# Row sums inverted in a compact tile by way of memory, part of their addition on GpSimd; norms, first taps and q/k scaling on ScalarE

## The chip, the cores and the metric

One core of a Trainium2 chip runs the whole kernel as one program. The metric is the device time of one execution in microseconds (us), less is better. The core has five engines with an instruction stream each: TensorE (PE in the profile; PEld is its weight load), VectorE (DVE), ScalarE (ACT), GpSimd (POOL) and SyncE (SP), which here only issues DMAs, all of them in one queue, in order. The engines meet through semaphores that the framework places. SBUF holds the tiles, PSUM the results of the matmuls, DRAM the inputs, the output and a few intermediate tiles.

## The reference, cut to what matters

x is (8, 256, 32, 32) in fp32: 8 images, 256 channels, 1024 positions. Four layers, each added to its input, x = x + layer(group_norm(x)):

```python
# layer 0: attention, 8 heads of 64; q and k of unit length over the head's channels
q, k, v = split(w_qkv @ gn(x));  q = q/|q|;  k = k/|k|
o = softmax(10 * q^T k) v;  y = w_out @ o + b_out
# layers 1 and 2: 3x3 convolution, 256 -> 256 channels, padding 1
# layer 3, after a layer norm over channels; 4 branches of 64 channels:
xm = mamba(xn) + skip_scale * xn       # causal conv of 4 taps, silu, 16-state scan over 1024 steps
g  = sigmoid(qpw @ conv3(xm));  xg = g * xm
R  = rpw @ conv3(xg) + xg
xm2 = fpw @ conv3(cat(xs, R)) + xs
out = gelu(layer_norm(fc @ cat(conv3(xm2), mha(xm2))))   # mha: 8 heads of 32 channels
out = proj @ layer_norm(dwconv3x3(norm_over_positions(out)))
```

What matters below: two softmaxes over 1024 keys per image, of which only the ratio (exp(s) v) / (sum of exp(s)) is wanted; norms, which are (x - mean) * rs per partition; and taps of depthwise convolutions, which are x * w + b for the first and an accumulation for the rest.

## The kernel before, in words

**Layout.** Channels lie on the 128 partitions, in two tiles; the 1024 positions lie along the free dimension, in two halves of 512 (`HALVES`). `work()` tiles (SBUF, 12 buffers) hold a 128x1024 image or more; `half_work()` tiles hold 512 columns. PSUM has two 128x1024 tiles (`big_tile`), one accumulator (`acc_tile`, 128x512) and two 512-column tiles for the scans (`da_tile`).

**Attention** (`attention`, L391 to L454) works on units: a pair of heads, a half of the queries and one of 8 key tiles; 4 pairs x 2 halves x 8 = 64 units per image and attention. For a unit, `scores` makes two matmuls into a big tile (L408) and ACT takes the exponential into a work tile p (L416); two units later `values` multiplies p with v into the accumulator, 64 rows for each of the two heads (L424). In layer 0 (`add_up`) DVE also adds the p tiles of the 8 key tiles up (the first addition L435, the others L438): 7 additions of 128x1024 per pair and half. After the last key tile the pair's `take` runs.

**Layer 0** (`layer0`): `rows_of` makes q and k of a pair (L488), copies them out of PSUM on DVE (L495), squares them on ACT with the sum beside it (L496), bounds the sum (L497), takes its power -1/2 on POOL (L180 in `inverse_root`), and scales on DVE (L499). Its `take` copies the accumulator to o (L542, ACT), sums the added p over the keys by a matmul with ones, which leaves the sum in all 64 rows of a head (L545), copies that to SBUF with a running sum for the overflow check (L554), takes the minimum (L389), the reciprocal of the 128x512 tile (L556) and multiplies (L557). The output projection (`project`, L309) reads the four o tiles.

**Mixer attention** (`mixer_attention`): v carries 32 columns of ones beside each head's 32 channels, so the accumulator has 32 rows of output and 32 rows of the sum for each head. `take` copies the output rows on DVE (L931) and the sum rows on ACT (L934), four copies of 32x512; once per four heads it takes minimum and maximum (L389, L941), the reciprocal of 128x1024 (L942), the product (L944) and a bias (L945).

**Norms and taps on DVE:** group norm (`group_stats` L207, `group_norm` L216), the first tap of `depthwise3` (L293), of the mamba's convolution (L664), of the 3x3 depthwise convolution and the norm ahead of it (`back_end`, L1068, L1078; the 8 other taps L1088), and the gate's (tanh + 1)/2 (L993).

**Scans** (in `scan_layers`): 4 branches x 2 halves x 4 groups of states. For one such step, SP loads dt, du (L732) and broadcast B and C rows (bc, L738), ACT makes exp(dt a) (L771), POOL multiplies du by B (L767, 128x2048), DVE scans 512 steps four times (L774), POOL multiplies by C (L784) and PE sums over states (L751).

**Order.** The program is written as streams of generators: the dense stream of an image (the rest of layer 3 of the image before, then layers 0 to 2 of the image after) is interleaved with the scans of the image at a given pace (L1156: 13.0, and 6.5 for the first and last image), and `overlap` joins the last layers of one image with the first of another. The framework then orders each engine's instructions by its own estimate of their times, within the dependences and the buffers. Each engine, and SP's queue, then works strictly in that order.

**At the end** the minima and maxima in `chk` decide by a flag (L1161 to L1172) whether an exact version of everything is run; with these inputs it isn't.

Of the kernel before, what the change touches and what calls it, by code (L numbers as in the profile page):

```python
# [31 lines left out]
def preact_stack(ctx: ExitStack, tc: tile.TileContext, I, out, cols):  # L32
# [136 lines left out]
    nc.vector.tensor_scalar_mul(moutw, moutw, 0.5)  # L169
# [22 lines left out]
    def group_stats(xt, psum):  # L192
# [18 lines left out]
        return g, rs  # L211

    def group_norm(xt, stats, dsts, view=lambda a: a):
        g, rs = stats
        for t in range(2):
            nc.vector.tensor_scalar(  # L216
                dsts[t],
                view(xt[:, t]),
                g[:, t, 0:1],
                rs[:, t : t + 1],  # L220
                ALU.subtract,
                ALU.mult,
            )
# [67 lines left out]
    def depthwise3(dst, src, wname, bname, i):  # L291

        nc.vector.tensor_scalar(  # L293
            dst, inner(src), col(wname, 3 * i + 1), col(bname, i), ALU.mult, ALU.add
# [84 lines left out]
    chk = wp.tile([P, 2, batch * 10], F32, name="chk")  # L379
    chk_at = [0]  # L380

    def note_at():
# [3 lines left out]
        return chk[:, 0, at : at + 1], chk[:, 1, at : at + 1]  # L386

    def least(dst, sums):
        nc.vector.tensor_reduce(dst, sums, axis=AX.X, op=ALU.min)  # L389

    def attention(pairs, add_up):  # L391
# [27 lines left out]
        def values(u):  # L419
# [11 lines left out]
            if add_up:  # L431
                if kt == 0:
                    pair["sum"] = u["p"]
                elif kt == 1:
                    nc.vector.tensor_add(u["p"], pair["sum"], u["p"])  # L435
                    pair["sum"] = u["p"]
                else:
                    nc.vector.tensor_add(pair["sum"], pair["sum"], u["p"])  # L438
            if kt == NKT - 1:
                pair["take"](h, pair["acc"], pair.get("sum"))  # L440
# [16 lines left out]
    def layer0(xt, exact=False):  # L457
# [22 lines left out]
        def rows_of(t, name, factor):  # L480
# [5 lines left out]
            for h in range(2):  # L486
# [8 lines left out]
            nc.vector.tensor_copy(a[:, 0:N], ps)  # L495
            nc.scalar.activation(ps, ps, AF.Square, accum_out=ss[:, 0:1])  # L496
            nc.vector.tensor_scalar_max(ss[:, 1:2], ss[:, 0:1], 1e-24)  # L497
            inverse_root(ss[:, 1:2])
            nc.vector.tensor_scalar(  # L499
                a[:, 0:N], a[:, 0:N], ss[:, 1:2], factor, ALU.mult, ALU.mult  # L500
            )
# [26 lines left out]
        def pair(t):  # L528
# [8 lines left out]
            def take(h, acc, total):  # L537
                if h == 0:
                    o_of[0] = work("o")
                    o.append(o_of[0])  # L540
                part = o_of[0][:, HALVES[h]]
                nc.scalar.copy(part, acc)  # L542
                ps = big_tile()
                for e in range(2):
                    nc.tensor.matmul(  # L545
# [742 lines left out]
```

## Time and profile before

| | |
|---|---|
| runs | 7,415.06 us median of 3 (7,414.7 to 7,417.16) |
| the profiled execution's own time | 7,415.1 us |
| its span in the profile | 7,413.3 us |
| granted TensorE clock, mean | 0.836 of full |
| a steady image | 885 us or so |
| DMAs | 419 MB, 57 GB/s in the mean |

How to read what follows. A profile is one execution. A line of a group gives the line of the kernel, engine, operation, output tile, inputs with shape, and count; then the total busy time and the mean of one in ns; then how long the engine had idled just before these instructions, with what ended most of it (`<-`). A window's row gives the busy time of each engine in a stretch of the span, with the clock that TensorE was granted, the busy share of the DMA engines and GB/s. A line of waits gives engine, line and tile, the engine, line and tile waited for, then us in total, times, and the longest. [...]

### The profile page before, as it was taken

What the parts mean: (1) busy time and instruction counts of PE and PEld (TensorE: products, weight loads), DVE (VectorE), ACT (ScalarE), POOL (GpSimd) and SP (SyncE); (2) the same over time, 40 slices, a digit from 0 to 9 for tenths busy, and PEclk for the clock granted to TensorE, in tenths of its full rate; (3) what the DMA queues carried; (4) which work ended last, traced back from release to release, by engine and by line L of the source; (5) the groups of instructions that cost most, each with busy time, mean ns of one, the idle gap of its engine ahead of it and who ended that gap; (6) DMA issues with size and microseconds to landing.
All of it is one profiled execution on the core that took longest, in us unless ns stands there. A gap on an engine that the chain in (4) does not pass through costs nothing. (4 is left out here: it accounts for less than half of the span.)

```text
span 7413.3 us, 50925 instructions
## 1 busy us (share of the span) xinstructions
PE 5914.4 (80%) x17602; PEld 2002.2 (27%) x17602; DVE 4468.7 (60%) x3907; ACT 2470.0 (33%) x3098; POOL 2753.4 (37%) x1093
## 2 busy tenths in 40 slices
PE   8987679778987889877898779978798788977276
PEld 2321222222322223222332223222242222312022
DVE  6278545587546874478554884558754687464533
ACT  3044214243153422434134331434315342143222
POOL 0035543335244351443524444234433435244510
PEclk9988778788877888878987889879898788877587
DMA  0022312122122222221212212222212222222200
GB/s 30 27 64 64 88 53 68 46 62 60 53 69 59 54 70 59 57 69 39 67 56 54 71 49 66 62 51 60 61 54 68 62 52 67 66 52 65 71 9 7
DMA packets 249190, 419.36 MB, mean 57 GB/s; under 512 B 49749, under 2 KB 93141, under 8 KB 246873
## 3 DMA queue, kind: packets, MB, share of 16 engines
q1 hardware_dynamic: 248920, 416.00, 21.2%
q8 instruction: 141, 2.31, 0.1%
q14 instruction: 129, 1.05, 0.0%
HBM read 361.28 MB, written 54.53 MB: 56 GB/s over the span
## 5 line engine op out<-in xcount | busy, mean ns | idle before, releaser
L784 POOL TENSOR_TENSOR hs<-hs,bc 128x2048 f32<-128x2048 f32 x256 | 1213.6, 4743 | 1465.4 <-issue 875.9
L767 POOL TENSOR_TENSOR hs<-du,bc 128x2048 f32<-128x2048 f32 x256 | 1196.9, 4684 | 698.4 <-PE y L751 433.3
L416 ACT ACTIVATE p<-big 128x1024 f32<-128x1024 f32 x1024 | 1040.8, 1020 | 958.7 <-PE big L408 887.3
L424 PE MATMUL acc<-p,v 128*64 128x512 f32 x4096 | 1290.8, 704 | 32.0 <-ACT rs L934 31.2
L771 ACT ACTIVATE da<-dt,a_neg 128x512 f32<-128x512 f32 x1024 | 700.8, 690 | 1759.8 <-DVE hs L774 1457.4
L606 PE MATMUL big<-im,w 128*128 128x512 f32 x2304 | 1061.4, 621 | 70.5 <-issue 70.0
L774 DVE TENSOR_TENSOR_SCAN hs<-da,carry,hs 128x512 f32<-128x512 f32 x512 | 624.9, 1264 | 465.5 <-POOL hs L767 453.0
L408 PE MATMUL big<-q,k 64*128 64x512 f32 x2048 | 688.4, 720 | 254.8 <-ACT p L416 131.3
L408 PE MATMUL big<-qk,qk 32*128 32x512 f32 x2048 | 695.8, 744 | 146.6 <-ACT p L416 145.9
L774 DVE TENSOR_TENSOR_SCAN hs<-da,hs 128x512 f32<-128x512 f32 x512 | 596.7, 1206 | 195.9 <-POOL hs L767 126.3
L438 DVE TENSOR_TENSOR p<-p 128x1024 f32<-128x1024 f32 x384 | 661.1, 1722 | 46.4 <-ACT p L416 22.4
L751 PE MATMUL y<-hs,sel 128*32 128x512 f32 x2048 | 363.9, 741 | 404.1 <-POOL hs L784 322.3
L606 PEld LDWEIGHTS big<-im,w 128*128 128x128 f32 x2304 | 452.0, 199 | 677.8 <-issue 674.3
L424 PEld LDWEIGHTS acc<-p,v 128*64 128x64 f32 x4096 | 237.4, 149 | 976.5 <-issue 828.6
L931 DVE COPY o<-acc 32x512 f32<-32x512 f32 x128 | 87.4, 683 | 515.3 <-PE acc L424 450.9
L408 PEld LDWEIGHTS big<-q,k 64*128 64x128 f32 x2048 | 185.6, 207 | 737.3 <-issue 250.8
L408 PEld LDWEIGHTS big<-qk,qk 32*128 32x128 f32 x2048 | 188.8, 212 | 639.2 <-ACT p L416 296.9
L309 PE MATMUL big<-o,w 128*128 128x512 f32 x384 | 200.1, 676 | 61.7 <-DVE o L945 61.7
L488 PE MATMUL big<-xn,w 128*128 128x512 f32 x512 | 229.3, 600 | 0.0
L751 PEld LDWEIGHTS y<-hs,sel 128*32 128x32 f32 x2048 | 50.1, 118 | 654.4 <-POOL hs L784 381.5
L556 DVE RECIPROCAL rs<-rs 128x512 f32<-128x512 f32 x64 | 214.4, 3350 | 1.9
L180 POOL TENSOR_TENSOR ln_r<-ln_r,minus_half 128x8 f32<-128x8 f32 x24 | 45.5, 1894 | 452.5 <-DVE ln_r L254 452.5
(203 smaller groups left out, 6016.6 us busy)
## 6 DMA issues: line engine op xcount, KB each, us to landing
bc<-bc SPq DMA_DIRECT2D x2048, 64.0 KB, 2.1
dt<-dt_m SPq DMA_DIRECT2D x256, 256.0 KB, 4.6
du<-du_m SPq DMA_DIRECT2D x256, 256.0 KB, 5.3
w<-in_wc SPq DMA_DIRECT2D x192, 192.0 KB, 2.4
dt_m<-dt SPq DMA_DIRECT2D x32, 512.0 KB, 2.6
du_m<-a SPq DMA_DIRECT2D x32, 512.0 KB, 2.8
xt<-in_x SPq DMA_DIRECT2D x8, 1024.0 KB, 5.0
w<-in_wqk SPq DMA_DIRECT2D x64, 128.0 KB, 2.1
```

The lines of the kernel that those rows point to most:

```text
L408: nc.tensor.matmul(s[:, HALVES[e]], pair["k"][e][:, kt * P : (kt + 1) * P], pair["q"][e][:, HALVES[h]], start=True, stop=True,)
L416: nc.scalar.activation(p, s, AF.Exp)
L424: nc.tensor.matmul(pair["acc"][e * 64 : e * 64 + 64], pair["v"][e](kt), u["p"][:, HALVES[e]], start=kt == 0, stop=kt == NKT - 1,)
L438: nc.vector.tensor_add(pair["sum"], pair["sum"], u["p"])
L488: nc.tensor.matmul(ps[:, HALVES[h]], w[:, c], xn[c][:, HALVES[h]], start=c == 0, stop=c == 1,)
L556: nc.vector.reciprocal(rs, rs)
L606: nc.tensor.matmul(image(ps[:, HALVES[h]]), w[:, dx], im[c][:, 16 * h + dy : 16 * h + dy + 16, dx : dx + 32], start=n == 0, stop=n == 17,)
L751: nc.tensor.matmul(y[g * 32 : g * 32 + 32], sel, hs[:, g], start=q == 0, stop=q == 3)
L767: nc.gpsimd.tensor_mul(hs, du, over_groups(b))
L771: nc.scalar.activation(da, dt[:, g], AF.Exp, scale=a_neg[:, at : at + 1])
L774: nc.vector.tensor_tensor_scan(hs[:, g], da, hs[:, g], 0.0 if h == 0 else carry[:, q, g : g + 1], ALU.mult, ALU.add,)
L784: nc.gpsimd.tensor_mul(hs, hs, over_groups(c))
```

## The change

- `invert` is new. It takes a DRAM tile of n rows of 1024 sums, loads it as a compact tile of 128 partitions x 8n columns, takes minimum and maximum into `chk` and the reciprocal there, stores it to DRAM, and reads each row back into as many partitions as a head has rows of output (64 or 32).
- Layer 0's `take` copies the ones-matmul's PSUM tile to SBUF, sends one row of each head to DRAM, and, once both halves of a pair are there, calls `invert` and multiplies o once over 128x1024.
- Of the additions of p, those of key tiles 3 and 5 go to a second total on GpSimd (it begins with key tile 1), the other four stay on DVE; the ones-matmul accumulates both totals, with four matmuls instead of two.
- The mixer's `take` copies the accumulator once on ACT; DMAs bring the output rows to o and one sum row of each head to DRAM; `invert` runs once per four heads. There are 76 more DMAs per image, 44 of them here.
- `rows_of` squares first, and its last step is an ACT pass from PSUM with the scale; the factor goes into the sum.
- Group norms, the norm in `back_end` and the first taps are ACT activations with scale and bias. The gate's pass goes into its multiplication, with constants changed in the weights.

```diff
--- before.py
+++ after.py
@@ -166,7 +166,11 @@
     nc.vector.tensor_scalar_mul(mxpw, mxpw, 0.5)
     nc.vector.tensor_scalar_mul(mxpw[:, :, 0:DS], mxpw[:, :, 0:DS], 0.5)
-    nc.vector.tensor_scalar_mul(moutw, moutw, 0.5)
+    nc.vector.tensor_scalar_mul(moutw, moutw, 0.25)
+    half_skip = wp.tile([P, 1], F32, name="half_skip")
+    nc.vector.tensor_scalar_mul(half_skip, col("skip"), 0.5)
+    nc.vector.tensor_scalar_mul(qdw, qdw, 2.0)
     half_d = wp.tile([P, NB], F32, name="half_d")
     nc.vector.tensor_scalar_mul(half_d, vec[:, cols["mD"] : cols["mD"] + NB], 0.5)
     half_qb = wp.tile([P, 2], F32, name="half_qb")
@@ -208,18 +212,21 @@
             rs, pd[:, 0:2], 1e-5, g[:, :, 1], ALU.add, ALU.add
         )
         inverse_root(rs)
-        return g, rs
+        shift = sp.tile([P, 2], F32, tag="shift", name="shift", bufs=4)
+        nc.vector.scalar_tensor_tensor(
+            shift, g[:, :, 0], -1.0, rs, ALU.mult, ALU.mult
+        )
+        return rs, shift
     def group_norm(xt, stats, dsts, view=lambda a: a):
-        g, rs = stats
+        scale, shift = stats
         for t in range(2):
-            nc.vector.tensor_scalar(
+            nc.scalar.activation(
                 dsts[t],
                 view(xt[:, t]),
-                g[:, t, 0:1],
-                rs[:, t : t + 1],
-                ALU.subtract,
-                ALU.mult,
+                AF.Identity,
+                bias=shift[:, t : t + 1],
+                scale=scale[:, t : t + 1],
             )
     def layer_norm(ts, sq, parts, small, finish):
@@ -290,8 +297,8 @@
     def depthwise3(dst, src, wname, bname, i):
-        nc.vector.tensor_scalar(
-            dst, inner(src), col(wname, 3 * i + 1), col(bname, i), ALU.mult, ALU.add
+        nc.scalar.activation(
+            dst, inner(src), AF.Identity, bias=col(bname, i), scale=col(wname, 3 * i + 1)
         )
         for k in (0, 2):
             nc.vector.scalar_tensor_tensor(
@@ -376,17 +383,30 @@
-    chk = wp.tile([P, 2, batch * 10], F32, name="chk")
+    chk = wp.tile([P, 2, batch * 6], F32, name="chk")
     chk_at = [0]
-    def note_at():
+    def invert(sums, n, dst, rows_each):
         at = chk_at[0]
         chk_at[0] += 1
-        return chk[:, 0, at : at + 1], chk[:, 1, at : at + 1]
-    def least(dst, sums):
-        nc.vector.tensor_reduce(dst, sums, axis=AX.X, op=ALU.min)
+        few = sp.tile([P, 4 * NKT], F32, tag="few", name="few")[:, 0 : n * NKT]
+        nc.sync.dma_start(
+            out=few, in_=sums.rearrange("n (p m) -> (n p) m", m=n * NKT)
+        )
+        nc.vector.tensor_reduce(chk[:, 0, at : at + 1], few, axis=AX.X, op=ALU.min)
+        nc.vector.tensor_reduce(chk[:, 1, at : at + 1], few, axis=AX.X, op=ALU.max)
+        nc.vector.reciprocal(few, few)
+        inv = dp.tile([n, N], F32, tag="inv%d" % n, name="inv")
+        nc.sync.dma_start(
+            out=inv.rearrange("n (p m) -> (n p) m", m=n * NKT), in_=few
+        )
+        for i in range(n):
+            nc.sync.dma_start(
+                out=dst[i * rows_each : (i + 1) * rows_each],
+                in_=inv[i : i + 1].to_broadcast([rows_each, N]),
+            )
     def attention(pairs, add_up):
@@ -429,15 +449,14 @@
                     stop=kt == NKT - 1,
                 )
             if add_up:
+                eng, n = (nc.gpsimd, 1) if kt in (1, 3, 5) else (nc.vector, 0)
                 if kt == 0:
-                    pair["sum"] = u["p"]
-                elif kt == 1:
-                    nc.vector.tensor_add(u["p"], pair["sum"], u["p"])
-                    pair["sum"] = u["p"]
-                else:
-                    nc.vector.tensor_add(pair["sum"], pair["sum"], u["p"])
+                    pair["sums"] = {}
+                total = pair["sums"].setdefault(n, u["p"])
+                if total is not u["p"]:
+                    eng.tensor_add(total, total, u["p"])
             if kt == NKT - 1:
-                pair["take"](h, pair["acc"], pair.get("sum"))
+                pair["take"](h, pair["acc"], pair.get("sums"))
         units = [
             {"t": t, "h": h, "kt": kt}
@@ -492,13 +511,13 @@
                         start=c == 0,
                         stop=c == 1,
                     )
-            nc.vector.tensor_copy(a[:, 0:N], ps)
-            nc.scalar.activation(ps, ps, AF.Square, accum_out=ss[:, 0:1])
-            nc.vector.tensor_scalar_max(ss[:, 1:2], ss[:, 0:1], 1e-24)
+            nc.scalar.activation(a[:, 0:N], ps, AF.Square, accum_out=ss[:, 0:1])
+            nc.vector.tensor_scalar(
+                ss[:, 1:2], ss[:, 0:1], 1e-24, factor**-2.0, ALU.max, ALU.mult
+            )
             inverse_root(ss[:, 1:2])
-            nc.vector.tensor_scalar(
-                a[:, 0:N], a[:, 0:N], ss[:, 1:2], factor, ALU.mult, ALU.mult
-            )
+            nc.scalar.activation(a[:, 0:N], ps, AF.Copy, scale=ss[:, 1:2])
             return a[:, 0:N]
         o = []
@@ -534,27 +553,34 @@
                 at = t * P + e * 64
                 return lambda kt: v[:, kt, at : at + 64]
-            def take(h, acc, total):
+            def take(h, acc, sums):
                 if h == 0:
-                    o_of[0] = work("o")
-                    o.append(o_of[0])
-                part = o_of[0][:, HALVES[h]]
-                nc.scalar.copy(part, acc)
+                    o_of["o"] = work("o")
+                    o.append(o_of["o"])
+                    o_of["sums"] = dp.tile([2, N], F32, tag="sums2", name="sums")
+                nc.scalar.copy(o_of["o"][:, HALVES[h]], acc)
                 ps = big_tile()
+                for n in range(2):
+                    for e in range(2):
+                        nc.tensor.matmul(
+                            ps[rows[e], 0:HALF],
+                            ones,
+                            sums[n][:, HALVES[e]],
+                            start=n == 0,
+                            stop=n == 1,
+                        )
+                rs = half_work("rs0")
+                nc.scalar.copy(rs, ps[:, 0:HALF])
                 for e in range(2):
-                    nc.tensor.matmul(
-                        ps[rows[e], 0:HALF],
-                        ones,
-                        total[:, HALVES[e]],
-                        start=True,
-                        stop=True,
+                    nc.sync.dma_start(
+                        out=o_of["sums"][e : e + 1, HALVES[h]],
+                        in_=rs[e * 64 : e * 64 + 1],
                     )
-                rs = half_work("rs0")
-                low, high = note_at()
-                nc.scalar.activation(rs, ps[:, 0:HALF], AF.Identity, accum_out=high)
-                least(low, rs)
-                nc.vector.reciprocal(rs, rs)
-                nc.vector.tensor_mul(part, part, rs)
+                if h == 1:
+                    r = work("rs0")[:, 0:N]
+                    invert(o_of["sums"], 2, r, 64)
+                    ot = o_of["o"][:, 0:N]
+                    nc.vector.tensor_mul(ot, ot, r)
             return {
                 "q": [q[r] for r in rows],
@@ -661,13 +687,12 @@
         yield
         u = mwork("u")
         uu = u[:, 0:N]
-        nc.vector.tensor_scalar(
+        nc.scalar.activation(
             uu,
             raw[:, 3 : 3 + N],
-            col("convw", 4 * i + 3),
-            col("convb", i),
-            ALU.mult,
-            ALU.add,
+            AF.Identity,
+            bias=col("convb", i),
+            scale=col("convw", 4 * i + 3),
         )
         for k in range(3):
             nc.vector.scalar_tensor_tensor(
@@ -812,7 +837,7 @@
             )
             part = inner(xn[j])[rows, HALVES[h]]
             nc.vector.scalar_tensor_tensor(
-                part, part, col("skip", 0, rows), ps[rows], ALU.mult, ALU.add
+                part, part, half_skip[rows], ps[rows], ALU.mult, ALU.add
             )
     def scan_layers(img):
@@ -915,7 +940,7 @@
             attention_exact(head(i) for i in range(8))
             return o
-        rs = {}
+        sums = {}
         def pair(i):
             t = i // 4
@@ -925,21 +950,22 @@
                 return lambda kt: v[:, kt, j]
             def take(h, acc, _):
-                if t not in rs:
-                    rs[t] = work("rs3")
+                if t not in sums:
+                    sums[t] = dp.tile([4, N], F32, tag="sums4", name="sums")
+                both = half_work("both")
+                nc.scalar.copy(both, acc)
                 for e in range(2):
-                    nc.vector.tensor_copy(
-                        o[t][rows[e], HALVES[h]], acc[e * 64 : e * 64 + 32]
+                    j, at = (i + e) % 4, e * 64
+                    nc.sync.dma_start(
+                        out=o[t][rows[e], HALVES[h]], in_=both[at : at + 32]
                     )
-                    nc.scalar.copy(
-                        rs[t][rows[e], HALVES[h]], acc[e * 64 + 32 : e * 64 + 64]
+                    nc.sync.dma_start(
+                        out=sums[t][j : j + 1, HALVES[h]],
+                        in_=both[at + 32 : at + 33],
                     )
                 if i % 4 == 2 and h == 1:
-                    r = rs[t][:, 0:N]
-                    low, high = note_at()
-                    least(low, r)
-                    nc.vector.tensor_reduce(high, r, axis=AX.X, op=ALU.max)
-                    nc.vector.reciprocal(r, r)
+                    r = work("rs3")[:, 0:N]
+                    invert(sums[t], 4, r, 32)
                     ot = o[t][:, 0:N]
                     nc.vector.tensor_mul(ot, ot, r)
                     nc.vector.tensor_scalar_add(ot, ot, col("ain_b", 4 + t))
@@ -988,9 +1014,8 @@
             nc.scalar.activation(
                 gate, ps, AF.Tanh, bias=half_qb[:, j : j + 1], scale=0.5
             )
-            nc.vector.tensor_scalar(gate, gate, 0.5, 0.5, ALU.mult, ALU.add)
             part = inner(xm[j])
-            nc.vector.tensor_mul(part, part, gate)
+            nc.vector.scalar_tensor_tensor(part, gate, 1.0, part, ALU.add, ALU.mult)
         yield 3.4
         xt = load_x(img["xd"])
@@ -1062,26 +1087,28 @@
         rs = sp.tile([P, 2], F32, tag="rs_hw", name="rs_hw")
         nc.vector.tensor_scalar_add(rs, mv[:, :, 1], 1e-5)
         inverse_root(rs)
+        shift = sp.tile([P, 2], F32, tag="shift_hw", name="shift_hw")
+        nc.vector.scalar_tensor_tensor(
+            shift, mv[:, :, 0], -1.0, rs, ALU.mult, ALU.mult
+        )
         dw = []
         for t in range(2):
             im = padded("dwim")
-            nc.vector.tensor_scalar(
+            nc.scalar.activation(
                 im[:, 1:33, 1:33],
                 image(xo[t]),
-                mv[:, t, 0:1],
-                rs[:, t : t + 1],
-                ALU.subtract,
-                ALU.mult,
+                AF.Identity,
+                bias=shift[:, t : t + 1],
+                scale=rs[:, t : t + 1],
             )
             dw.append(work("dw")[:, 0:N])
             acc = image(dw[t])
-            nc.vector.tensor_scalar(
+            nc.scalar.activation(
                 acc,
                 im[:, 1:33, 1:33],
-                col("dwc_w", 9 * t + 4),
-                col("dwc_b", t),
-                ALU.mult,
-                ALU.add,
+                AF.Identity,
+                bias=col("dwc_b", t),
+                scale=col("dwc_w", 9 * t + 4),
             )
             for k in (0, 1, 2, 3, 5, 6, 7, 8):
                 dy, dx = k // 3, k % 3
```

## The prediction, made before the changed kernel ran

> **What bounds the kernel now.** I read the page from the top. Section 1 first:
>
> ```profile
> span 7413.3 us, 50925 instructions
> PE 5914.4 (80%) x17602; PEld 2002.2 (27%) x17602; DVE 4468.7 (60%) x3907; ACT 2470.0 (33%) x3098; POOL 2753.4 (37%) x1093
> ```
>
> TensorE (PE) leads, yet 1,499 us of the span have no matmul. The 40 slices show PE at 6 to 9 tenths in a pattern that repeats about every five slices, one image, so the question is which stage lets PE idle. I took the matmuls in time order, cut them where the source line changes, and asked for the busy time of every engine in the stages of an image. A steady image (2 to 6) lasts some 885 us.
>
> In each row: window, its length, busy us of PE, PEld, DVE, ACT, POOL, granted clock.
>
> ```profile
> 31.00:209.00 178.00, 169.53 (x611) 47.30 (x610) 119.03 (x102) 83.69 (x103) 4.34 (x8) 0.99 0.04 11
> 3256.00:3537.00 281.00, 214.32 (x710) 55.78 (x708) 238.18 (x169) 122.40 (x159) 120.67 (x35) 0.85 0.21 58
> 3804.00:4007.00 203.00, 175.31 (x577) 41.97 (x576) 78.14 (x71) 108.15 (x126) 86.95 (x22) 0.81 0.29 73
> 7152.00:7290.00 138.00, 129.80 (x506) 33.19 (x508) 20.52 (x20) 73.54 (x78) 0.00 (x0) 0.99 0.00 1
> ```
>
> Rows 1 and 2 are the first attention (layer 0) of image 0, alone, and of image 4, beside the scans of image 3. Alone, PE works 95% of the time. Beside scans the stage takes 103 us more: PE 76%, **DVE 85%**, ACT 44%, POOL 43%. DVE (VectorE) bounds it. Rows 3 and 4 are the mixer's attention with and without scans: there DVE is at 38%, PE at 86%.
>
> What keeps DVE busy, from the groups kept apart by shape (last columns: total, mean ns, idle before and its releaser):
>
> ```profile
> L438 DVE TENSOR_TENSOR p<-p 128x1024 f32<-128x1024 f32 x384 | 661.1, 1722 | 46.4 <-ACT p L416 22.4 <-DVE p L438 0.5
> L435 DVE TENSOR_TENSOR p<-p 128x1024 f32<-128x1024 f32 x64 | 156.1, 2438 | 20.4 <-ACT p L416 16.4 <-PE acc L424 4.0
> L556 DVE RECIPROCAL rs<-rs 128x512 f32<-128x512 f32 x64 | 214.4, 3350 | 1.9
> L942 DVE RECIPROCAL rs<-rs 128x1024 f32<-128x1024 f32 x16 | 104.8, 6553 | 0.5
> L216 DVE TENSOR_SCALAR im<-xt,g,rs 128x1024 f32<-128x1024 f32 x32 | 120.9, 3819 | 12.3 <-POOL rs L180 12.3
> ```
>
> The same add has a median of 1.22 us and a mean of 1.72. The timeline (start, length, instruction) shows why:
>
> ```profile
> 3416.97 5.48 POOL L767 TENSOR_TENSOR hs<-du,bc 128x2048 f32<-128x2048 f32 x1
> ...
> 3418.02 5.52 DVE L438 TENSOR_TENSOR p<-p 128x1024 f32<-128x1024 f32 x1
> ...
> 3426.99 1.22 DVE L438 TENSOR_TENSOR p<-p 128x1024 f32<-128x1024 f32 x1
> ```
>
> An add that meets a scan multiply on POOL is stretched to about the length of the multiply; the group norm before a convolution (L216 im, 0.79 at its least, median 4.98) likewise. So DVE's busy time holds waiting for POOL.
>
> **The change, stage by stage.** The engine sums first. DVE loses three of seven adds of each head pair and half (3/7 of 817 = 350 us), reciprocals (319, less about 15 for compact ones), their reductions (some 80), q/k copies and scalings (L495, L499: 155), norms (L216: 158), mixer copies (L931: 87) and first taps (about 120): some 1,250 of 4,469 us. ACT gains some 275 us, POOL 128 adds at 2.35 (L625, the same shape on POOL) = 301, PE 128 more ones-matmuls (L545's 79.6 us again = 80, 10 per image). SP issues 608 more DMAs. What counts is where an engine ends a stage.
>
> *Layer 0's attention beside scans (images 1 to 7).* In the second window DVE drops 3/7 of 105.5 us of adds (45), eight reciprocals (26.8, compact ones left 2: 25), reductions (4), the halved multiplies (3), and q/k copies and scalings (20): 97, leaving 141 of 281 us. Now 43 us of the stage are not DVE; 141 + 43 = 184 would be its new end, below PE's 214 + 10 = 224. With PE's 95% from row 1 that is 236. But POOL has 24 adds x 2.35 = 56 on its 121, so 177, and the adds that stay on DVE (32 x 1.22 = 39) exclude POOL: 216 of mutually exclusive time, as much as now (121 + 56 x 1.22 + q/k work = 210). The bounds are therefore 236 (PE alone) and 281 or a little more (nothing won); I take 243, near the PE row, because no chain is serial through all three: **-38**, range -50 to +10.
>
> *q and k.* The two DVE passes become one ACT pass (128x1024 with a scale: 1.11 to 1.24 us by L1041 and L278), after POOL's power. ACT must wait between Square and Copy; behind it queue the exponentials. Today's DVE waits there are 71 us over 64 tiles (L499), 1.1 us each, 8.9 per image if none hides; the PSUM tile, one of two, stays held. **+4**, range -2 to +16.
>
> *End of that attention.* Now: L545 to L557 take 7.5 us, mostly under the output projection's first three inputs. After: ACT copies 0.6, two DMAs of sums issued (0.8) and landed (2), load of the compact tile (0.4 + 2), DVE about 0.6, store (0.4 + 2), two broadcasts (0.8 + 2.1), multiply 1.2 = 13; landings are those of "bc<-low" (1.9) and "bc<-bc" (2.1), issue 0.4 from SP's rows. 6 uncovered, and SP issues in order, with scan loads between: **+9**, range +3 to +30. The other three pairs' inversions lie under the next pair's units, 281 / 4 = 70 us.
>
> *Convolution entries.* At 3558.41 DVE needs 9.97 us for two im's because POOL multiplies; PE starts at 3563.58. ACT needs 1.2 for the first: -3.5 twice, **-7**. If ACT were behind exponentials or scan work, one such instruction (1.0) is lost; range -8 to 0.
>
> *Mixer's attention (images 0 to 6).* A take now alternates four copies on DVE and ACT, about 3.1 us with the only accumulator held; after, one copy of 0.6. PE waits 31.2 us for ACT at L424, ACT 72.1 us for DVE there: 3.9 and 9 per image, so 0 to -13; **-9**. At its end the chain of 13.9 us (four copies, reductions 2.4, reciprocal 6.5, multiply, add) becomes copy 0.6, four DMAs 3.6, load 2.4, 0.6, store 2.4, four broadcasts 3.7, DVE 1.8 = 15.1, and a queue in which SP has bc loads of the scans between the steps: **+8**, range +1 to +30.
>
> *First taps, gate.* In the last stage 3.8 us of serial DVE work (L1068, L1078) become 2.4 on ACT, and the gate's pass goes: **-3**, range -5 to +2. Depthwise and convw taps move from one idle-rich engine to another: nothing; if the cover is gone, 12 x 0.3 us.
>
> **Sum.** Images 2 to 7: (-38 + 4 + 9 - 7) x 6 = -192. Image 1's attention runs beside image 0's scans, where everything up to 1,064 us is stretched by them (its convolutions take 145 and 128 us instead of 67), so what it wins is waited for later: 0. Mixer side (-9 + 8 - 3) x 7 = -28. Image 0's first layer, at 95% PE: +8 (matmuls) +9 (end) = +17. Tail: -5. Together -208 on the profiled execution's 7,415.1 (span 7,413.3, so 1.8 outside it), which equals the median of 7,415.06: **7,207**.
>
> [...]
>
> **Rivals.**
> - *PE's limit is reached.* Attention falls to 231 us beside scans (224 at 97%), in all seven images, without the added waits, the mixer's by 20: -50 x 7 - 20 x 7 - 42 + 17 = -515, 6,900. For: PE at 95% alone. Against: the clock granted beside scans is 0.81 to 0.85, not 0.99.
> - *The exclusion bounds it.* 216 us of DVE adds and POOL work stay, in POOL's strict order; p buffers wait for POOL's adds behind 4.7-us multiplies. The stage wins only 12: (-12 + 4 + 9 - 7) x 6 - 28 + 12 = -52, 7,363.
> - *SP's order makes it slower.* One mechanism: the dependent DMAs of the last inversion of each attention stand in SP's queue behind scan loads that wait for their buffers.
>
> ```profile
> SPq L738 <- POOL hs L784: 1418.0, 154, 31.9
> SPq L738 <- POOL hs L767: 674.9, 108, 22.0
> ```
>
>  Such a wait is 9.2 us in the mean (1418/154). Two inversions per image on the path, three steps each: 2 x 3 x 9.2 = 55, of which I counted 10; 45 x 7 - 208 = +107, 7,522. It decides from two such waits in three steps (30 us per image eat the gain). Against: about 345 scan-load waits stand among some 2,850 DMAs, one in eight.
> - *Nothing to measure:* the DVE time was cover, 7,400 to 7,430.
>
> **Numbers.** A measurement of this kernel can tell about 0.2% (15 us) from no change. Forecast (7,100 to 7,320) 0.46; PE's limit (6,860 to 7,050) 0.12; exclusion (7,330 to 7,395) 0.18; no change 0.07; slower 0.17. Faster 0.46 + 0.12 + 0.18 = 0.76. The range of 6,980 to 7,450 leaves out half of the first rival and most of the slower case, 0.06 + 0.13.
>
> **What would show it.** Right: in the window of layer 0's attention DVE under 160 us, the stage 235 to 255 us; L216's successor at 1.2 us and PE starting each convolution 3 us sooner; o's multiply 13 to 20 us after the last accumulation. Wrong: the stage stays above 265 us with POOL above 180 and DVE adds of 4 us and more (exclusion); or SP waits between the load and the broadcasts of 10 us and more while PE idles before the output projections (SP's order); or ACT waits for POOL's power with PE idle at the scores (q/k step).

## The result, and the profile after

The changed kernel takes 7,758.21 us (median of 4, 7,748.8 to 7,766.03) against 7,415.07: **4.6% slower**, ratio 1.0462, 95% interval 1.0443 to 1.048; its profiled execution took 7,748.8. Its page opens so:

```profile
span 7747.0 us, 52208 instructions
...
PE 6321.8 (82%) x17858; PEld 2067.9 (27%) x17858; DVE 3554.7 (46%) x3213; ACT 2733.5 (35%) x3241; POOL 3088.2 (40%) x1221
```

DVE lost 914 us of work (some 1,250 were forecast), and the kernel is 334 us longer. PE is 407 us busier, though the 256 added records of the ones-matmul account for only 67 (146.9 us against 79.6). So the same matmuls have become slower (a value matmul took 704 ns in the mean, now 789). The windows say where (columns: window, length, busy us of PE, PEld, DVE, ACT, POOL, **granted clock**, DMA share, GB/s): layer 0's attention beside scans, the mixer's attention beside scans, and the mixer's attention of the last image, alone.

```profile
3460.00:3718.00 258.00, 209.93 (x726) 55.96 (x724) 152.66 (x108) 122.40 (x149) 139.89 (x45) 0.91 0.23 59
3989.00:4237.50 248.50, 242.38 (x578) 51.38 (x577) 59.93 (x56) 105.50 (x120) 82.76 (x22) 0.58 0.24 62
7493.00:7625.00 132.00, 131.68 (x512) 31.94 (x512) 3.87 (x6) 68.94 (x71) 0.00 (x0) 1.00 0.05 13
```

Set beside the rows of before: layer 0's attention fell from 281 to 258 us, but the mixer's rose from 203 to 248.5 with PE busy for 98% of it and the clock down from 0.81 to 0.58. Alone, the same mixer attention got *faster*, 140 to 132, at clock 1.00. A steady image went from 885 to 942 us: mixer's attention +45, from its end to the next layer 0 attention +32 (133 to 165), layer 0's attention -23, the rest +3 to +8. Part of the -23 belongs with the +32: of the scans' steps (counted by the y matmuls), layer 0's attention now holds 8 instead of 10, and the stretch before it 7 instead of 5.

The clock is the first thing to understand. In both traces it has two levels, 0.50 and 1.00, and changes only on a grid of 3.41 us: of its 410 stretches before and 378 in the changed kernel, all but the last one of each trace are whole multiples of that. PE in the mixer's attention of the kernel before, and below it the windows of the grid at the same moment, with the value matmuls (L424) alone (window, length, busy us and records of PE, then of PEld, granted clock, DMA share, GB/s):

```profile
3828.82 2.08 PE L408 MATMUL big<-qk,qk 32*128 32x512 f32 x4
3830.83 1.98 PE L424 MATMUL acc<-p,v 128*64 128x512 f32 x4
3832.74 3.79 PE L408 MATMUL big<-qk,qk 32*128 32x512 f32 x8
3836.60 3.23 PE L424 MATMUL acc<-p,v 128*64 128x512 f32 x8
3839.76 1.13 PE L408 MATMUL big<-qk,qk 32*128 32x512 f32 x4
```

```profile
3832.41:3835.82 3.41, 0.40 (x2) 0.00 (x0) 0.50 1.01 209
3835.82:3839.23 3.41, 2.63 (x8) 0.76 (x8) 0.50 0.96 211
3839.23:3842.65 3.42, 1.67 (x8) 0.20 (x4) 1.00 0.59 122
```

Four score records take 2.08 us at half clock and 1.13 at full. With the regular pattern of four and four the clock stays at 0.50 (in the two windows ahead of these, 3825.58 to 3832.41). At 3832 the pattern breaks: DVE's copies L931 and ACT's L934 are taking the accumulator out by turns, from the first to the last of these lines,

```profile
3832.85 0.68 DVE L931 COPY o<-acc 32x512 f32<-32x512 f32 x1 [6.50 <-PE acc L424]
...
3835.97 0.58 ACT L934 COPY rs<-acc 32x512 f32<-32x512 f32 x1
```

so PE makes the scores of two units, then the values of two, eight records in one window, and the next window has the full clock. In the changed kernel, in the same attention:

```profile
4024.96 2.08 PE L428 MATMUL big<-qk,qk 32*128 32x512 f32 x4
4026.97 1.98 PE L444 MATMUL acc<-p,v 128*64 128x512 f32 x4
4028.88 2.08 PE L428 MATMUL big<-qk,qk 32*128 32x512 f32 x4
```

Here PE does not pause and stays at half clock (0.50 without a gap for 99 us from 4001.0 on): a unit takes 3.9 us instead of 2.07 (before, alone, 7161.33 to 7163.40), and 64 x 3.9 = 250 us would be the whole stage (its mean clock is 0.58, so a small part ran at full clock). I had two causes to choose from. Waits of the changed kernel (engine and line, what it waited for, us, times, longest):

```profile
POOL hs L792 <- DMA du<-du_m: 270.3, 7, 43.1
```

```profile
SPq L959 <- ACT both L956: 767.9, 62, 26.9
```

SP stands 768 us for the copies of the mixer's takes, and behind it the scans' du loads come late, once per image, by 39 us in the mean, so the scans' own matmuls are missing from PE for that long (over the whole stage they are as many as before: 578 records of PE against 577). **Theory 1:** that is what keeps the clock down. **Theory 2:** the fast release of the accumulator takes the bunches away, whatever SP does.

### The profile page after: what moved, and what is told of

Same layout as the page of the kernel before. It is cut to its first block, busy times and chain, and to the rows that moved or that the text cites. A ratio compares the mean times of both kernels' runs of the same rounds, so it can differ in the third digit from the quotient of the medians.

```text
span 7747.0 us, 52208 instructions
## 1 busy us (share of the span) xinstructions
PE 6321.8 (82%) x17858; PEld 2067.9 (27%) x17858; DVE 3554.7 (46%) x3213; ACT 2733.5 (35%) x3241; POOL 3088.2 (40%) x1221
## 5 line engine op out<-in xcount | busy, mean ns | idle before, releaser
L809 POOL TENSOR_TENSOR hs<-hs,bc 128x2048 f32<-128x2048 f32 x256 | 1187.0, 4639 | 983.7 <-issue 390.8
L444 PE MATMUL acc<-p,v 128*64 128x512 f32 x4096 | 1448.8, 789 | 5.3 <-ACT o L561 3.4
L428 PE MATMUL big<-qk,qk 32*128 32x512 f32 x2048 | 903.9, 953 | 6.9 <-ACT p L436 6.2
L428 PE MATMUL big<-q,k 64*128 64x512 f32 x2048 | 643.4, 696 | 161.4 <-ACT p L436 76.9
L457 DVE TENSOR_TENSOR p<-p 128x1024 f32<-128x1024 f32 x256 | 570.1, 2227 | 407.0 <-ACT p L436 362.9
L457 POOL TENSOR_TENSOR p<-p 128x1024 f32<-128x1024 f32 x128 | 353.0, 2758 | 429.8 <-ACT p L436 428.8
L428 PEld LDWEIGHTS big<-qk,qk 32*128 32x128 f32 x2048 | 227.3, 263 | 692.4 <-ACT p L436 338.9
L565 PE MATMUL big<-p,ones 128*64 128x512 f32 x512 | 146.9, 696 | 115.3 <-DVE p L457 115.3
L184 POOL TENSOR_TENSOR rs<-rs,minus_half 128x2 f32<-128x2 f32 x32 | 22.5, 704 | 533.0 <-DVE rs L211 460.7
```

The lines of the kernel that those rows point to most:

```text
L428: nc.tensor.matmul(s[:, HALVES[e]], pair["k"][e][:, kt * P : (kt + 1) * P], pair["q"][e][:, HALVES[h]], start=True, stop=True,)
L444: nc.tensor.matmul(pair["acc"][e * 64 : e * 64 + 64], pair["v"][e](kt), u["p"][:, HALVES[e]], start=kt == 0, stop=kt == NKT - 1,)
L457: eng.tensor_add(total, total, u["p"])
L565: nc.tensor.matmul(ps[rows[e], 0:HALF], ones, sums[n][:, HALVES[e]], start=n == 0, stop=n == 1,)
L809: nc.gpsimd.tensor_mul(hs, hs, over_groups(c))
```

## The experiments

Each ratio is to the kernel before on the same chip, with its interval. The intervals are 0.3 to 0.6% wide. The kernel before took 7,413 to 7,428 us on the chips of these runs, so times of different chips compare to some 15 us.

**1. The mixer's take of before, all else changed.**

```diff
-                both = half_work("both")
-                nc.scalar.copy(both, acc)
...
-                    r = work("rs3")[:, 0:N]
-                    invert(sums[t], 4, r, 32)
+                    nc.vector.tensor_copy(
+                        o[t][rows[e], HALVES[h]], acc[e * 64 : e * 64 + 32]
+                    )
+                    nc.scalar.copy(
+                        rs[t][rows[e], HALVES[h]], acc[e * 64 + 32 : e * 64 + 64]
+                    )
...
+                    nc.vector.reciprocal(r, r)
```

> The changed kernel with the mixer's take of before (DVE and ACT copies, reciprocal on DVE) and all else of the change. Theory (the mixer's take, whose DMAs wait in SP's queue in front of the scans' du loads, stalls the scans and with that leaves TensorE at half clock in the mixer's attention): attention there back from 248 to about 203 us, the wait behind it from 41 to 10 us, in seven images: 7758 - 7 x 76 = about 7,225 us (7,180 to 7,270). Rival (the smoother stream of matmuls, or the other parts' work on ACT and POOL, brings the half clock): attention stays near 240, only the wait behind it goes: about 7,540.

Measured: 7,355.9, ratio 0.9918 (0.9901 to 0.9934). The mixer's attention is back at 207 us, the wait behind it at 15 (until the projection takes the second o; 46 in the changed kernel; counted from the last value matmul, so 5 us more than the expectation's 10 and 41). So the loss lies in the mixer's take, 7,758 - 7,356 = 402 us, and the rest of the change is worth only -0.8%; I had expected more of it because I had taken layer 0's -23 us for its own. With the take of before, layer 0's attention holds 10 scan steps again and lasts 270: the real gain is 11.

**2. The mixer's take alone, in the kernel before** (the same lines the other way round).

> The kernel before with the changed mixer's take alone. Theory: the mixer's attention rises from 203 to about 248 us and the wait behind it by 31, in seven images: 7,415 + 7 x 76 = about 7,950 us (7,850 to 8,000). Rival (it takes the other parts for the half clock): 7,415 + 7 x 31 = about 7,630.

Measured: 7,784.13, ratio 1.049 (1.0473 to 1.0508). The mixer's attention takes 262 us at clock 0.55 and the wait behind it 44: it needs none of the other parts. The total lies between the two numbers, since layer 0's attention, one scan step lighter, gave back 13 us per image.

**3. The take's DMAs issued by ScalarE.**

```diff
-                    nc.sync.dma_start(
+                    nc.scalar.dma_start(
                         out=o[t][rows[e], HALVES[h]], in_=both[at : at + 32]
                     )
```

(and the same for the sums.)

> The changed kernel with the four DMAs of each mixer's take issued by ScalarE after its copy, not by SP. Theory: SP no longer stands still for the copies, du loads come in time, the scans go on, attention back to 205 us or less: 7758 - 7 x 45 = about 7,440 us (7,400 to 7,490); the wait behind the attention stays. Rival (it is the regular stream of matmuls without DVE's copies, whatever the scans do): 7,700 or more.

Measured: 7,731.57, ratio 1.0428 (1.0411 to 1.0446). In the image I followed, POOL's first scan multiply starts 40 us into the attention (4,006 us, the attention begins at 3,966) instead of 67 (4,056 and 3,989 in the changed kernel); in the kernel before it was 39 (3,843 and 3,804). Yet the stage lasts 242 to 249 us at clock 0.60 to 0.61. Theory 1 fails here, though not cleanly: SP then waited 388 us for these DMAs in front of its bc loads.

**4. Scores over 128 rows.**

```diff
-                "q": [qk[t][r, 0:N] for r in rows],
-                "k": [qk[2 + t][r, 0:N] for r in rows],
+                "q": [qk[t][:, 0:N] for r in rows],
+                "k": [qk[2 + t][:, 0:N] for r in rows],
```

> The changed kernel with the scores of the mixer's attention made over all 128 rows of q and k instead of a head's 32: as many matmuls of as many columns, but the heads are not kept apart, so the result is not the reference's. Theory that the half clock itself makes the 45 us, and that it stays because 32-row matmuls with the value matmuls alone are too little work to raise it: granted clock near 1 in the mixer's attention, attention 205 us or less with SP and the scans held up as they are: about 7,440 us (7,380 to 7,480). Rival (the clock is a symptom: PE would wait for the scans anyway): attention still 235 to 250, 7,680 to 7,760.

Measured: 7,591.97, ratio 1.0235 (1.0218 to 1.0252). Its mixer attention beside scans, and alone:

```profile
3877.40:4091.80 214.40, 204.14 (x578) 60.44 (x577) 60.08 (x56) 104.84 (x120) 82.97 (x22) 0.98 0.28 72
7284.50:7470.90 186.40, 186.40 (x514) 56.32 (x512) 3.89 (x6) 69.20 (x71) 0.00 (x0) 1.00 0.03 9
```

The clock beside scans is 0.98 (0.96 to 0.98 in six images), with the same takes, DMAs and SP queue: the stage falls by 34 us although the experiment made PE's work longer, which I had overlooked. Alone the stage takes 186 us instead of 132: at full clock four records of 128 rows take 1.98 us, where those of two heads in 32 rows each took 1.13. In the traces the records of the two heads start 0.007 us apart on 32 rows and 0.43 to 0.53 us apart on 128: they ran beside each other before. The half clock is a cause and not a symptom.

**5. Four copies kept, sums through memory.** The take of experiment 1 with, after each pair of copies, a DMA of one row of sums, and `invert` in place of the reciprocal:

```diff
+                    nc.sync.dma_start(
+                        out=sums[t][j : j + 1, HALVES[h]],
+                        in_=rs[t][j * 32 : j * 32 + 1, HALVES[h]],
+                    )
...
-                    nc.vector.reciprocal(r, r)
+                    invert(sums[t], 4, r, 32)
```

> The changed kernel, but the mixer's take makes the four copies of before (output rows on DVE, sum rows on ACT, the accumulator held for some 3 us), and only the sums go by DMA through memory to the compact inversion. New theory, after the DMAs on ScalarE won 27 us alone: before, the held accumulator makes PE run ahead with scores and then do eight value matmuls in one clock window, which raises the clock again; the fast release takes these bunches away, and PE stays at half clock. It expects the mixer's attention near 205 to 215 us with the long wait behind it kept (about 46): 7,356 + 7 x 31 = about 7,570 us (7,480 to 7,620). Rival (SP's queue, standing for the takes, holds the scans' loads, and the missing sums over states keep the clock down): attention 235 or more, 7,680 or more.

Measured: 7,501.25, ratio 1.0088 (1.0069 to 1.0107). The mixer's attention is 207 us (217 in one of the first six images) with DMAs in SP's queue; the wait behind it is 39. Held accumulator, clock back:

```profile
3863.70:4070.70 207.00, 182.20 (x578) 43.86 (x578) 79.67 (x70) 109.12 (x127) 87.62 (x22) 0.79 0.26 71
```

**6. Four wide matmuls more per take.**

```diff
+                ps = big_tile()
+                for m in range(4):
+                    nc.tensor.matmul(
+                        ps[:, HALVES[m % 2]],
+                        qk[2 + t][:, 0:P],
+                        qk[t][:, HALVES[m % 2]],
...
+                    )
```

> The changed kernel with four matmuls of 128x128 by 512 columns more per mixer's take, into a PSUM tile that nobody reads: work added, nothing taken away. Theory (too little of the array at work in a window keeps the half clock): the clock rises at each take, the attention falls to about 203 + 8 x 2 = 220 us, total 7,758 - 7 x 28 = about 7,560 us (7,480 to 7,640). Rival (half clock is not what costs): 7,758 + 7 x 16 to 28 = 7,870 to 7,950.

Measured: 7,640.88, ratio 1.0276 (1.0248 to 1.0304). Work was added and 117 us were won (1.9% by the two ratios). The mean clock of the whole run rises from 0.795 to 0.845, but eight takes per attention do not hold it up all the time (230 to 243 us), so less than I expected.

**7. The kernel before, accumulator released after one copy, no DMA.**

```diff
+                both = half_work("both")
+                nc.scalar.copy(both, acc)
                 for e in range(2):
                     nc.vector.tensor_copy(
-                        o[t][rows[e], HALVES[h]], acc[e * 64 : e * 64 + 32]
+                        o[t][rows[e], HALVES[h]], both[e * 64 : e * 64 + 32]
                     )
```

> The kernel before, but the mixer's take copies the accumulator once on ACT and makes the four copies of before from that copy: the accumulator is released in 0.6 us, and there are no new DMAs. Theory of the held accumulator: attention from 203 to between 235 and 262 us, about 7,700 us (7,620 to 7,830). Rival (SP's queue): no DMA, so 203 us and 7,415 within 40.

Measured: 7,665.64, ratio 1.032 (1.0299 to 1.0342). This decides it. No new DMA, the wait behind the attention as before (14.5), and a stage of 227 to 254 us with the four-and-four pattern of the changed kernel:

```profile
3927.90:4181.70 253.80, 234.98 (x578) 50.00 (x577) 86.64 (x71) 112.57 (x133) 87.02 (x22) 0.60 0.23 59
```

With two levels, a mean of 0.60 means 2 x (1 - 0.60) = 80% of 254 us at half clock, 203 us; before, 0.81 gave 77 of 203. So 126 us more at half clock cost 51 us.

The one place shown above stands for the rest. Counted over the traces of six kernels, in the seven mixer attentions beside scans: of the 3.41-us windows at half clock in which only scores and one to four value records start, 7 of 1,337 were followed by full clock; with six or more value records, 60 of 72. Such fuller windows number 19, 20 and 28 where the accumulator is held (before, 1, 5), and 1, 0 and 4 where it is released fast (changed kernel, 2, 7). Most other rises have the scans' sums over states in the window: 25 of all 42 before, 15 of 22 after.

The fast release does not lower the clock by itself: alone, the changed kernel's stage stays at 1.00 for its 132 us. None of the 486 full-clock windows with six or more value records was followed by half clock; all 198 falls came after windows with four or fewer. What the release takes away beside scans is the way back.

**8. The best parts:** experiment 1, the last head pair of layer 0 inverted in halves as before, and the shift of the norms computed otherwise:

```diff
-        nc.vector.scalar_tensor_tensor(
-            shift, g[:, :, 0], -1.0, rs, ALU.mult, ALU.mult
-        )
+        for t in range(2):
+            nc.vector.tensor_scalar(
+                shift[:, t : t + 1], g[:, t, 0:1], rs[:, t : t + 1], -1.0,
+                ALU.mult, ALU.mult,
+            )
...
+                if t == 3:
...
+                    nc.vector.reciprocal(rs, rs)
```

> The changed kernel with the mixer's take of before (as in the first experiment, 7,356), the last head pair of layer 0 inverted in its halves as before, and the norm's shift computed by two one-column tensor_scalar with one tensor input each in place of the one with two (median 4.44 us for 2 columns beside POOL's scan multiplies). Expected: the wait behind layer 0's attention back by 10 us, the shift at 0.2 us each and so each convolution 3 to 4 us earlier: 7,356 - 7 x 17 = about 7,240 us (7,210 to 7,290). Rival (the shift is late for another reason, or stays shut out): only the 10 us, about 7,285 to 7,300.

Measured: 7,256.07, ratio 0.9763 (0.9746 to 0.978). The shift in the changed kernel and here (the view of one line: durations in ns least/median/most):

```profile
L216 DVE SCALAR_TENSOR_TENSOR shift<-g,rs x32: 160/4443/4446, 15.2 to 6747.6; 128x2 f32<-128x2 f32 x32
```

```profile
L217 DVE TENSOR_SCALAR shift<-g,rs x64: 177/205/216, 14.6 to 6237.0; 128x1 f32<-128x1 f32 x64
```

Two columns cost 4.44 us, because the instruction follows POOL's power and POOL then starts a scan multiply: the 20 that took 4.44 us each started 0.06 to 0.07 us into such a multiply of 4.49 us and ended 0.02 us before it did, the 12 that took 0.16 ran beside none. With one tensor input and a scalar pointer it is not held up: 26 of the 64 run beside such a multiply, and the longest of all took 0.216 us. The entries of the convolutions fall from 12.8 and 14.1 us (as in experiment 1) to 8.0 and 10.3, PE's gap ahead of the projection's last input from 9 us to under 1.

Experiments 9 to 12 take single parts back from this kernel.

**9. All additions on DVE**, `eng, n = nc.vector, 0`, and two ones-matmuls per half.

> The best kernel so far (the one of the eighth experiment, ratio to before 0.976, 7,256 us) with all seven additions of p on DVE again, in one total, and two ones-matmuls. Prediction's step (relieving DVE of 45 us per image shortens layer 0's attention): 10 to 20 us more in each of six images, 7,310 to 7,380 us, ratio 0.985 to 0.995. Rival (GpSimd's adds and DVE's exclude each other, so nothing is won): 7,200 to 7,265, PE even saves 10 us of matmuls per image.

Measured: 7,255.02, ratio 0.9785 (0.9772 to 0.9799). GpSimd's additions win nothing that can be seen: 7,255 against 7,256 us (the ratios differ because the kernel before took 7,413 us on this chip and 7,428 on that of experiment 8). The adds of experiment 8, then of 9:

```profile
L468 DVE TENSOR_TENSOR p<-p 128x1024 f32<-128x1024 f32 x256 | 575.0, 2246 | 313.0 <-ACT p L447 307.6 <-DVE p L468 0.5
...
L468 POOL TENSOR_TENSOR p<-p 128x1024 f32<-128x1024 f32 x128 | 367.3, 2869 | 317.3 <-ACT p L447 314.0 <-DMA bc<-bc 1.8
```

```profile
L468 DVE TENSOR_TENSOR p<-p 128x1024 f32<-128x1024 f32 x448 | 770.8, 1721 | 329.0 <-ACT p L447 228.3 <-PE acc L455 83.7
```

**10. No inversion of layer 0 by way of memory**, `if t >= 0:` in place of `if t == 3:`.

> The same best kernel with all head pairs of layer 0 inverted in their halves on DVE as before, none by way of memory. Prediction's step (20 us of DVE per image in the reciprocals of three pairs lie on the path): 7,256 + 6 x 10 to 20 = 7,310 to 7,380 us. Rival (those reciprocals lay in DVE's idle time, or the DMAs cost as much): 7,230 to 7,270.

Measured: 7,257.74, ratio 0.9789 (0.9775 to 0.9802): nothing either, on the same chip as 9.

**11. q and k on DVE**, the six lines of `rows_of` as before.

> The same best kernel with q and k copied and scaled on DVE as before. Prediction's step (20 us of DVE per image saved, 4 lost to ACT's wait): 7,256 + 6 x 5 to 15 = 7,290 to 7,350 us. Rival (ACT's wait and the longer hold of the PSUM tile cost as much as DVE wins): 7,200 to 7,260.

Measured: 7,301.49, ratio 0.9848 (0.9835 to 0.9862): layer 0's attention takes 277 us instead of 271. Moving q and k to ACT is worth about 45 us, by experiment 8 and by 9 and 10 on the same chip.

**12. Experiments 9 and 10 together.**

> The same best kernel (7,256 us, ratio 0.976) with both taken back at once: all additions of p on DVE in one total, and all inversions of layer 0 on DVE in halves. Alone, neither made a difference. Theory that either one frees DVE enough and the other is then idle-time relief: with neither, DVE is at 210 to 220 of layer 0's 270 us and bounds it again, 5 to 10 us per image in six images: 7,285 to 7,320 us, ratio 0.983 to 0.988. Rival (DVE is not the bound of that attention at all since q and k left it): 7,245 to 7,265 us.

Measured: 7,210.8, ratio 0.9716 (0.9703 to 0.9729), the fastest of all. Neither expectation holds. Layer 0's attention beside scans is 272.7 us against 271, so DVE (214 of 272.7 us) costs 2 us there; image 0's, alone, is 175.6 against 185.4. The rest comes from a stage the edit doesn't touch, the mixer's attention of images 1 to 5: experiment 8, then 12.

```profile
3714.60:3922.00 207.40, 182.26 (x578) 43.01 (x577) 79.91 (x70) 108.84 (x127) 86.89 (x22) 0.78 0.27 72
```

```profile
3689.00:3888.40 199.40, 170.62 (x569) 41.06 (x569) 81.85 (x72) 107.49 (x127) 85.73 (x22) 0.83 0.30 76
```

Eight us in each of five images, some 40 of the 45, go with the clock; image 0's 10 and layer 0's 2 in each of six images about cancel. Experiment 11 has one such image (199.7) beside five of 207.5 in the same execution, so the stage can take either time without any edit, and I would not count this much as a gain. What decides between the two no run shows.

## Why the prediction was wrong

The forecast was 7,207 and faster; the kernel is 4.6% slower, outside the range. By its steps:

- **Mixer's attention, "-9, range 0 to -13": +45. This is the step that failed.** The wait priced was there and went: alone, the stage fell by 8 us. But I had taken PE's time per matmul as given. PE's rows in both windows showed 0.81 and 0.99, and I read the 0.81 as the price of running beside scans. It went with PE's own pattern: with the rows of the scores alone changed the clock was 0.98 instead of 0.58 (4), with the release of the accumulator alone changed 0.60 instead of 0.81 (7). The take's hold of the accumulator, which I costed as a loss, was what raised the clock: released fast, with DMAs (2, clock 0.55) or without (7, 0.60), the stage takes 227 to 262 us; held, with DMAs (5, 0.79) or without (1), 207. Experiment 7 gives 3.2% for this alone, about 240 of the 402 us.
- **Its end, "+8, range +1 to +30": +31** (15 to 46 us), 24 with the accumulator held (5). I added up DMAs, and these went as reckoned: the store was issued as the reciprocal ended, at 4257.9, and the broadcasts 1.85 us later. What I missed is DVE's order. On DVE at the end of the mixer's attention:

```profile
4247.64 4.45 DVE L216 SCALAR_TENSOR_TENSOR shift<-g,rs 128x2 f32<-128x2 f32 x1 [0.81 <-POOL rs L184]
...
4253.20 0.17 DVE L398 TENSOR_REDUCE chk<-few 128x1 f32<-128x32 f32 x1
...
4253.39 4.23 DVE L832 TENSOR_TENSOR u<-u,z 128x1024 f32<-128x1024 f32 x1
4257.54 0.34 DVE L400 RECIPROCAL few<-few 128x32 f32<-128x32 f32 x1
...
4274.88 1.20 DVE L970 TENSOR_TENSOR o<-o,rs 128x1024 f32<-128x1024 f32 x1
...
4277.26 4.98 DVE L971 TENSOR_SCALAR o<-o,vec 128x1024 f32<-128x1024 f32 x1
```

  The compact tile's load was issued at 4241.3. Each return to DVE falls behind work that had been far off when the chain stayed on DVE: the reductions wait until 4253, the reciprocal of 0.34 us until 4257, the product until 4275. A chain of DMAs lets the scans' steps in between (7 instead of 5 before the next attention).
- **Layer 0's attention, "-38": -11 like for like** (270 against 281 with 10 scan steps each, experiment 1); 12 of the -23 were scan steps put elsewhere. DVE's busy time fell to 153 of 258 us with 8 scan steps, but to 177 of 270 with 10, not to the 141 forecast; at 85% it had bound the stage by only some 11 us. What is left is PE waiting at each pair's end (16 us in the window above, L565 for the adds) and for the scans (8 us).
- **GpSimd's additions.** The second rival had this right and I gave it 0.18: in experiment 8 the adds left on DVE went from 1.72 to 2.25 us in the mean and those on POOL took 2.87, not 2.35, so 196 us less on DVE were bought with 367 on POOL, and no time (9). In the kernel before, too, adds were drawn out beside POOL: the 89 of the 384 at L438 that met a scan multiply took 4.39 us in the median, the other 295 took 1.23.
- **q and k, "+4" after -20 of DVE:** the move pays, as forecast, but 6 us per image in this attention (277 against 271), about 45 in all (11), not 16. The +4 alone was not measured.
- **End of layer 0's attention, "+9": +10.** Right, and doing the last pair on DVE takes most of it back (8).
- **Convolution entries, "-7": 1 to 6 us worse.** Before, the first took 7.4 or 11.6 us and the second 13.4 to 13.8; now 12.6 to 12.8 and 14.1. The norm on ACT takes 1.24 us, as reckoned, but the two-input shift ahead of it was counted as nothing, by its two columns. The 4.44 us are the multiply's length, not that of two columns. Experiment 8, with 8.0 and 10.3, has some 5 us of the gain the step spoke of.
- **Back layers "-3":** the stretch between the second convolution and the mixer's attention fell from 91 to 94 us to 86, and that from the mixer's attention to the next image from 133 to 130 (1, scan steps alike). The forecast was low; no run takes these parts back singly.
- **Third rival (SP's order, 0.17):** right in sign, not in mechanism. SP did stand still, but for the takes, with the scans' loads behind it, and freeing it (3) won 27 us.

What stays open: what exactly raises the granted clock. The runs show that back-to-back matmuls are not enough: in six attentions of the changed kernel PE worked without a gap for 99 to 126 us at 0.50, and each time the last window ahead of the rise held four or eight matmuls of the scans' sums over states. The clock also rose with wider matmuls, in 4 (128 rows in place of 32: 0.58 to 0.98 in the stage) and in 6 (four more of 128x128 per take: 0.795 to 0.845 over the run), but no run tells apart which property of a matmul does it.

## What to carry to other kernels

Before a stage is called bound by PE or by waiting, read the granted clock of its windows and ask which pattern of matmuls holds it; shortening a wait can take away the bunch of work that kept the clock up (here 0.81 became 0.58, and 203 us 248.5). Price a step moved to another engine or queue by what stands in front of each of its returns (here +31 us where +8 was forecast), and count a tiny instruction at the length of what it may have to wait out, not at its size (here 4.44 us beside a multiply of 4.49, for 0.16). When a stage gets shorter beside another stream, count that stream's steps in it before calling it a gain.

## What I had not expected of the hardware

- At full clock, score matmuls of two heads on 32 rows each take 1.13 us for four records, on 128 rows 1.98: on different rows they overlap, their starts 0.007 us apart (on 128 rows 0.43 to 0.53; 4).
- Half clock lasted under a full queue, 99 to 126 us at a time at 0.50 in the changed kernel, and full clock under the same pattern, 132 us at 1.00 alone; a stage beside scans took 248.5 us at a mean of 0.58; in experiment 7 from 227 to 254 us between images of the same execution.
- An instruction on two columns took 4.44 us in the median beside POOL's scan multiply; the same sums with a scalar pointer took 0.2, never more than 0.22 in 64.
